# One of four block additions in a seven-product matrix multiplication done by an adding DMA, with the work of every half step laid out anew

## The chip, the cores and the metric

The kernel runs on one core of a Trainium2 chip, in float32. The metric is device time in microseconds (us) of one execution, as the median of several runs. Engines are named as in the profile: PE is TensorE (matmuls; PEld its weight loads), DVE is VectorE, ACT is ScalarE, POOL is GpSimd, and SP issues most of the DMAs.

## The reference

There are 16 batches (graphs) of 1024 nodes with 128 features, and two layers. The input adjacency is 0 or 1.

```python
# layer 0, per batch
h = x @ Ww.T + Wb
e = (h @ A) @ h.T;  e = e + e.T
attention = softmax(where(adj > 0, e, 0), axis=1) * adj
h_prime = relu(attention @ h)
ic, fc, oc = sigmoid(h_prime @ w?_u + x @ w?_x)      # three gates per node
x = layernorm(x + oc * tanh(ic * h_prime + fc * x))
# layer 1, per batch and head (4 heads)
h = x @ conv_w[hd] + conv_b[hd]
scores = h @ attn_w[hd] @ h.T
hh = relu(tanh(adj * scores) @ h)
x = layernorm(x + relu(relu(mean(hh over heads)) + x))
```

## The kernel before

Nodes are cut into 8 blocks of 128 rows, and rows of 1024 columns into 2 halves of 512. The main loop runs over the 16 batches `b`. In iteration b the kernel does layer 1 of batch b, and spread between its steps it does the end of layer 0 of batch b+1, the beginning of layer 0 of batch b+2 (pieces with a leading `+` in the plan), and the end of layer 1 of batch b-1 (`e`).

**Layer 1 in steps.** A batch has 4 heads x 8 steps. Two steps make a `Pair` (`i` = 0 to 3 in a head): a step multiplies one block of 128 rows by the head's matrix to get 128 x 1024 scores (two matmuls of 128 x 512 into PSUM, from a ring of three score buffers), DVE multiplies them by the adjacency out of PSUM into the pair's SBUF tile (L821 for the first half of the pair, L819 with a factor -1 for the second), and ACT takes tanh of the 128 x 1024 (L826).

**Seven products.** In batches 0 to 14, heads 0 to 2 are "fast": the product of the tanh matrix with h is done as a 2 x 2 block product with seven multiplications in place of eight (Winograd's form). The pair tile has five parts of 512 columns, in the order X3, N21, B22, B11, N12. The first half's scores fill B11 and N12, the second half's fill N21 and B22. Four block additions follow on DVE: `differ` makes X3 = N12 + B22 and N12 = N12 + B11 in one instruction of 1024 columns (L830), `differ_more` makes B22 = B22 + N12 (L892) and then N21 = B22 + N21 (L893). The seven products (L853) are

- P1: B11 with a block of h; P2: N21 as it was with h; P3: B22 as it was with hx; these are "early", and they sum in one PSUM tile over the four pairs of a head;
- P5: the new N12 with hx; P7: X3 with h; P4: the new N21 with h; P6: the new B22 with hx; these are "late", in another PSUM tile.

hx are three sums and differences of h's blocks that POOL makes (`join_rows`, L786 to L789). At the end of a head, `early_second` copies the early sums out of PSUM on ACT (L902, L905), `combine` joins them with the late ones on DVE (L912 to L917), `sum_up` adds on POOL (L924) and takes relu on ACT (L928, L930), and `sum_end` adds the head to the sum on POOL (L936). Head 3 and batch 15 multiply plainly (L865 in the fast batches).

**When a pair is worked on, before.** Pair p of a batch has its scores in steps 2p and 2p+1. The main loop holds two older pairs, `before` (p-1) and `old` (p-2). `differ` comes at the end of step 2p+2, the early products in step 2p+3 (P3 and P2 behind the first 512 scores, P1 behind the second), `differ_more` at that step's end, and the late products in step 2p+4 (P5, P7 behind the first 512 scores, P4, P6 behind the second).

**What sets the order.** There is no scheduler: each engine works through its instructions in the order in which the Python code issues them. The other work is laid out by hand in `PLAN` (and `FIRST` for b = 0), 64 strings for a batch's 64 half steps. `slot(n)` runs the pieces of string n: 2 x step after the first 512 scores of a step, 2 x step + 1 at its end. The pieces that the texts below name are: L load an adjacency block on SP; S scores of layer 0 and T their transposition through DRAM (a "hop": SP writes, and `land` reads back at the end of the step); E finds the edges (L466, POOL, 128 x 1024); A masks (L483, DVE) and takes exp (ACT); B weighs (L516, DVE) and multiplies; P to V are the gates and the normalization of layer 0. Of the gates, `weigh_hp` multiplies on POOL (L610), `sum_hp` sums on DVE (L616, L618), and `forget` multiplies x by the forget gate on POOL (L629, 128 x 1024). r and u make h and the head's matrix for layer 1, j calls `join_rows`, D turns the new x. The batch's output goes out by a DMA that POOL issues (L1033).

Of the kernel before, what the change touches and what calls it, by code (L numbers as in the profile page):

```python
# [15 lines left out]
ALU = mybir.AluOpType  # L16
# [3 lines left out]
P = 128  # L20
# [4 lines left out]
def two_layer_adjacency_kernel(  # L25
# [19 lines left out]
    nc = tc.nc  # L45
    B, N, D = x.shape
    H = conv_w.shape[0]
    assert D == P and N % 512 == 0
    NB = N // P
    NH = N // 512  # L50
    BH = NB // NH
# [287 lines left out]
    def layer0(b):  # L339
# [5 lines left out]
        t = {}  # L345
# [280 lines left out]
        def forget():  # L626
            t["u"] = sb.tile([P, NB, D], F32, tag="u", name=f"u0_{b}", bufs=1)
            t["x1"] = sb.tile([P, NB, D + 1], F32, tag="x1", name=f"x1_{b}")
            nc.gpsimd.tensor_mul(  # L629
                t["u"], t["x"], t["gate"][:, :, 1:2].to_broadcast([P, NB, D])  # L630
            )
            nc.gpsimd.memset(t["x1"][:, :, 0:1], 1.0)

        def gate_f():
# [61 lines left out]
        else:  # L696
            pieces.update(
                P=turn_hp, Y=partial(weigh_hp, 1), F=gate_f, f=gate_f_end, i=gate_i, o=gates_io,
# [104 lines left out]
    class Pair:  # L803
# [30 lines left out]

        def product(self, p):
            b, hd, i = self.b, self.hd, self.i
            if i == 0 and p == 3:
                early = ps_acc.tile([P, N], F32, tag="acc1", name=f"early_{b}_{hd}")
                acc1_t[b, hd] = {2: early[:, :HN], 1: early[:, HN:512], 3: early[:, 512 : 512 + HN]}
                acc1_t[b, hd, 0] = early  # L840
            if i == 0 and p == 5:
                late = ps_acc.tile([P, N], F32, tag="acc2", name=f"late_{b}_{hd}")
                for n, r in enumerate((5, 7, 6, 4)):
                    acc1_t[b, hd][r] = late[:, ts(n, HN)]
            out = acc1_t[b, hd][p]
            h, x = h1_t[b, i // 2][:, i % 2], hx_t[b, hd, i // 2][:, :, i % 2, :]
            d1, d2 = slice(hd * D, hd * D + HD), slice(hd * D + HD, (hd + 1) * D)
            w, at = {
                1: (h[:, 0, d1], B11), 2: (h[:, 1, d1], N21), 3: (x[:, 2], B22),
                4: (h[:, 1, d2], N21), 5: (x[:, 0], N12), 6: (x[:, 1], B22), 7: (h[:, 0, d2], X3),  # L850
            }[p]
            for q in range(NH):
                nc.tensor.matmul(  # L853
                    out[ts(q, HD)], w, self.t[:, at, ts(q, HN)],
                    start=(i == 0 and p in (2, 3, 5, 4)), stop=(i == BH - 1),
                    skip_group_check=True,
                )

# [16 lines left out]
                for e in range(2):  # L875
                    add_head(b, hd, acc1_t[b, hd][:, ts(e, 512)], e * 512)

        def late_first(self):
            self.product(5)
            self.product(7)  # L880

        def late_second(self):
            self.product(4)
            self.product(6)

        def early_first(self):
            self.product(3)
            self.product(2)

        def differ_more(self):  # L890
            t = self.t
            nc.vector.tensor_add(t[:, B22], t[:, B22], t[:, N12])  # L892
            nc.vector.tensor_add(t[:, N21], t[:, B22], t[:, N21])  # L893

        def early_second(self):
            self.product(1)
            if self.i < BH - 1:
                return
            b, hd = self.b, self.hd
            w = acc1_t[b, hd, 1] = sb.tile([P, 6, HN], F32, tag="w", name=f"w_{b}_{hd}", bufs=1)  # L900
            early = acc1_t[b, hd, 0]
            nc.scalar.copy(  # L902
                w[:, 4::-4, :], early[:, :512].rearrange("p (k n) -> p k n", k=2)
            )
            nc.scalar.copy(w[:, 5, :], early[:, 512 : 512 + HN])  # L905

        def combine(self):
            if self.i < BH - 1:
# [199 lines left out]
    for g in range(2):  # L1108
# [2 lines left out]


    PLAN = [
        "u1.1 B2", "B3", "A4 L5", "", "E5 r2 B4 r3", "r6 A5", "", "L6 E6", "L7 A6",
        "E7 u1.0 e B5", "", "r7", "B6 A7 j0.1", "B7", "", "e", "R0", "G0 G1 j1.0 j1.1",
        "G2 G3 G4", "+W", "G5 e", "G6 e", "G7 R1 e", "e P u2.0", "e +L0", "+E0 +H0 +h0", "",
        "j2.0", "+Q0", "u2.1 e", "Y", "+L1 +Q1", "+H1 +h1", "e X F", "u3.0 j2.1", "+S0 f", "+T0",
        "+H2 +h2 i +S1 +T1", "+S2 j3.0", "+T2 +S3", "o", "+S4 I0", "I1", "+T3 +S5", "", "",
        "+E1 O0", "u3.1", "+A0 O1", "+S6", "+B0 +L2 Va", "Vb Vc", "", "j3.1 Vd +T4 +L3 N0",
        "D +S7", "+A1", "+E2", "+T5", "+A2", "+B1 +E3", "", "", "r5 u0.1 u0.0 r4 +A3 r0 r1",  # L1120
        "+T6 +L4 +E4 j0.0",
    ]

    FIRST = [
        "A0", "B0 S5 L3", "E1 A1", "u1.1 E2 T3", "S6 T4 E3", "B1 A2 L4", "B2 u1.0 L5 T5", "E4 A3",
        "", "B3", "A4", "B4 E5", "S7 L6 L7 T6", "A5", "", "j1.1", "", "E6 X B5 E7", "A6 j1.0",
        "B6 A7 +W", "B7", "", "R0", "G0 G1 G2 G3 G4 G5", "G6 u2.1 G7 +L0", "+E0 +H0 +h0 R1", "P",
        "", "+Q0", "", "", "u2.0 +L1 +Q1", "j2.0 +H1 +h1", "Y F", "", "+S0", "j2.1 +T0",
        "+H2 +h2 f +S1 +T1", "+S2", "i +T2 +S3", "u3.0", "+S4", "u3.1 o", "+T3 I0 +S5", "",
        "O0 I1", "+E1", "j3.0 O1", "+A0 j3.1", "+S6 Va", "+B0 +L2", "Vb Vc", "Vd", "N0 +T4 +L3",  # L1130
        "D +S7", "+A1", "+E2", "+T5", "+A2", "+B1 +E3", "", "", "r1 u0.1 r4 +A3 r0 u0.0 r5",
        "+T6 +L4 j0.0 +E4",
    ]
    begun.append(True)
    end, nxt, ended = None, second, None
    pairs = deque([None, None])
    for b in range(B):
        plan = PLAN if b else FIRST
        after = layer0(b + 2) if b + 2 < B else {}

        def slot(n):
            for name in plan[n].split():
                if name == "e":
                    if end is not None:
                        next(end, None)
                elif name == "D":
                    if b + 1 < B:
                        turn_x1(b + 1)
                elif name[0] in "rju":
                    c = b + (n >= H * NB if name[0] == "r" else name[1] == "0" and n >= H * NB)  # L1150
                    if c == B:
                        continue
                    if name[0] == "r":
                        rows(c, (int(name[1]),))
                    elif name[0] == "j":
                        join_rows(c, int(name[1]), int(name[3]))
                    else:
                        head_uT(c, int(name[1]), [int(name[3])])
                elif name[0] == "+":
                    run(after, name[1:])  # L1160
                else:
                    run(nxt, name)

        for step in range(H * NB):
            hd, m = divmod(step, NB)
            i, half = divmod(m, 2)
            old, before = pairs
            if b + 1 < B:
                if half == 0:
                    now = Pair(b, hd, i)  # L1170
                for q in range(NH):
                    now.score(half, q)
                    if half == 0 and old and old.fast:
                        (old.late_second if q else old.late_first)()
                    if before and not before.fast:
                        before.plain(half, q)
                    elif half and before:
                        (before.early_second if q else before.early_first)()
                    if half and q == 0 and old and old.fast:
                        old.combine()  # L1180
                    if q == 0:
                        slot(2 * step)
                now.tanh(half)
                if half and before and before.fast:
                    before.differ_more()
            else:
                now = None
                layer1_step(b, hd, m)
                slot(2 * step)
                if half == 0 and old and old.fast:  # L1190
                    old.late_first()
                    old.late_second()
                if before and not before.fast:
                    before.plain(half, 0)
                    before.plain(half, 1)
                elif half and before:
                    before.early_first()
                    before.early_second()
                    before.differ_more()
                if half and old and old.fast:  # L1200
                    old.combine()
            if half == 0 and before and before.fast:
                before.differ()
            land()
            if half and old and old.fast:
                old.sum_up()
            if half == 0 and ended and ended.fast:
                ended.sum_end()
            slot(2 * step + 1)
            if step > H * NB - NB and b + 1 < B:  # L1210
                load_adj1(b + 1, ORDER[m - 1])
# [4 lines left out]
            if half:  # L1216
                ended = old
# [65 lines left out]
```

## Time and profile before

| | |
|---|---|
| runs | 2413.98 us median of 3 (2413.82 to 2415.39) |
| the execution profiled | 2419.07 us |
| its span, first to last instruction | 2417.2 us, mean granted TensorE clock 0.999 |
| L821, L819 DVE, scores times adjacency, 128 x 512 | 480 each, 677 and 679 ns |
| L826 ACT, tanh, 128 x 1024 | 480, 1056 ns |
| L853 PE, late and early products | 5 groups of 720 or 1440 records, 379 to 384 ns |
| L466 POOL, edges | 120, 2945 ns |
| L610 POOL, weighing | 45, 2496 ns |
| L629 POOL, forget gate | 15, 1908 ns |
| L513 ACT, multiplication of 128 x 128 by a column | 124, 398 ns |
| L1033 POOL, issue of the output DMA, 512 KB | 15, 1.01 us; 3.9 to 4.5 us from issue to landing |
| DMA traffic | 261 MB, mean 108 GB/s |

The page gives, for each group of instructions, the busy time in all, the mean time of one, and the idle time of the engine just before them with what ended most of it. A matmul has two records per instruction, and the two instructions of one 128-column matmul work on the two halves of the array at once; their ends are modelled, so the mean of a record is longer than the time for which it holds PE. The batches from 1 to 13 are alike, with a period of 147.5 to 149.0 us.

### The profile page before, as it was taken

The numbers are of one execution on the slowest core, as the hardware profiler recorded it, in microseconds if no ns is written. First come the engines' busy times: TensorE is split into PE (matmuls) and PEld (weight loads), VectorE is DVE, ScalarE is ACT, GpSimd is POOL, SyncE is SP. The second block draws the span as 40 slices with busy tenths as digits, with TensorE's granted clock in tenths as the row PEclk, the third lists the DMA queues.
The fourth block names the chain that finished last, engine by engine and source line by source line (L and its number), as shares of the span: only waits on it lengthen the run. The fifth ranks groups of instructions, "written<-read, shape, count | busy, mean of one in ns | idle before, by whom it ended". The sixth has DMA issues, their size and how long they took to land.

```text
span 2417.2 us, 37283 instructions
## 1 busy us (share of the span) xinstructions
PE 2364.2 (98%) x13817; PEld 1016.6 (42%) x13817; DVE 2032.3 (84%) x3682; ACT 1215.1 (50%) x1992; POOL 963.1 (40%) x713
## 2 busy tenths in 40 slices
PE   9899999999999999999999999999999999999999
PEld 5343433434354343544435434343443434434334
DVE  7888897988889888998888979889798897988645
ACT  6545454554545545455454554545445454564443
POOL 1544444444344443445434354344444434444100
PEclk9999999999999999999999999999999999999999
DMA  4525243452524425235252343524335243441200
GB/s 141 131 71 157 79 114 114 102 158 72 132 95 118 151 76 151 84 98 162 76 169 79 104 133 90 163 79 106 122 97 157 79 127 101 109 154 44 88 27 9
DMA packets 461783, 260.98 MB, mean 108 GB/s; under 512 B 387107, under 2 KB 412450, under 8 KB 461603
## 3 DMA queue, kind: packets, MB, share of 16 engines
q1 hardware_dynamic: 459149, 250.68, 36.9%
q0 software_dynamic: 2160, 7.87, 1.1%
q8 instruction: 109, 1.79, 0.3%
q14 instruction: 71, 0.58, 0.1%
q10 hardware_dynamic: 294, 0.07, 0.0%
HBM read 199.04 MB, written 59.51 MB: 107 GB/s over the span
## 4 chain that ended last, share of the span: by engine, by line
PE 63%; DVE 30%; DMA 2%; issue 2%; ACT 1%; POOL 1%; SPq 0%; DVEq 0%; POOLq 0%; ACTq 0%
PE sc L78 24%; PE acc L78 10%; PE late L853 8%; PE acc L865 6%; PE early L853 5%; DVE pair L819 4%; DVE pair L830 4%; PE pR L78 4%; DVE pair L821 3%; PE pT_u L78 3%; DVE pair L893 3%; DVE pair L892 3%; DVE turn L441 2%; DVE hws L616 2%; DVE R L483 2%
## 5 line engine op out<-in xcount | busy, mean ns | idle before, releaser
L78 PE MATMUL sc<-uT,x1T 128*64 128x512 f32 x4096 | 1057.5, 595 | 17.9 <-DVE h L402 5.1
L826 ACT ACTIVATE pair<-pair 128x1024 f32<-128x1024 f32 x480 | 506.7, 1056 | 581.0 <-DVE pair L821 332.5
L78 PEld LDWEIGHTS sc<-uT,x1T 128*64 128x64 f32 x4096 | 292.0, 137 | 448.3 <-issue 231.3
L819 DVE SCALAR_TENSOR_TENSOR pair<-sc,adj 128x512 f32<-128x512 f32 x480 | 321.2, 679 | 170.7 <-PE sc L78 169.1
L466 POOL TENSOR_SCALAR edge<-ring 128x1024 uint8<-128x1024 f32 x120 | 352.9, 2945 | 272.8 <-DMA ring<-in_adjT_dram 248.5
L821 DVE TENSOR_TENSOR pair<-sc,adj 128x512 f32<-128x512 f32 x480 | 318.0, 677 | 72.5 <-PE sc L78 70.7
L865 PE MATMUL acc<-pair,h 128*64 128x512 f32 x960 | 248.1, 594 | 0.0
L78 PE MATMUL acc<-R,h 128*64 128x512 f32 x960 | 240.5, 592 | 3.2 <-issue 1.6
L495 ACT ACTIVATE R<-R,nmax 128x1024 f32<-128x1024 f32 x126 | 144.5, 1147 | 195.1 <-DVE nmax L491 191.1
L853 PE MATMUL late<-pair,h 128*64 128x256 f32 x1440 | 221.0, 384 | 15.3 <-DVE pair L893 13.5
L241 POOL TENSOR_TENSOR rs<-rs,mhalf 128x8 f32<-128x8 f32 (+3 forms) x35 | 54.1, 1546 | 432.0 <-DVE rs L238 431.9
L830 DVE TENSOR_TENSOR pair<-pair 128x1024 f32<-128x1024 f32 x180 | 225.8, 1254 | 0.0
L853 PE MATMUL late<-pair,hx 128*64 128x256 f32 x1440 | 218.3, 380 | 0.1
L853 PE MATMUL early<-pair,h 128*64 128x256 f32 x1440 | 217.8, 379 | 0.0
L483 DVE CUSTOM_DVE_ANT_0 R<-R,edge 128x1024 f32<-128x1024 f32 x120 | 168.4, 1403 | 7.5 <-POOL edge L466 6.0
L893 DVE TENSOR_TENSOR pair<-pair 128x512 f32<-128x512 f32 x180 | 164.9, 916 | 6.2
L924 POOL TENSOR_TENSOR w<-w 128x512 f32<-128x512 f32 x45 | 57.4, 1275 | 279.1 <-ACT hpT L538 215.9
L853 PEld LDWEIGHTS late<-pair,h 128*64 128x64 f32 x1440 | 101.1, 137 | 157.7 <-DVE pair L893 71.2
L853 PEld LDWEIGHTS late<-pair,hx 128*64 128x64 f32 x1440 | 105.9, 137 | 127.0 <-issue 92.6
L853 PEld LDWEIGHTS early<-pair,h 128*64 128x64 f32 x1440 | 105.9, 137 | 126.3 <-issue 101.5
L516 DVE TENSOR_TENSOR R<-R,ring 128x1024 f32<-128x1024 f32 x120 | 154.8, 1290 | 0.0
L892 DVE TENSOR_TENSOR pair<-pair 128x512 f32<-128x512 f32 x180 | 149.4, 830 | 0.0
(215 smaller groups left out, 2939.6 us busy)
## 6 DMA issues: line engine op xcount, KB each, us to landing
adj<-in_adjT_dram SPq DMA_DIRECT2D x128, 512.0 KB, 4.5
ring<-in_adjT_dram SPq DMA_DIRECT2D x120, 512.0 KB, 4.9
xT<-in_xT_dram SPq DMA_DIRECT2D x16, 512.0 KB, 4.8
x<-in_x_dram SPq DMA_DIRECT2D x16, 512.0 KB, 7.6
dram_hp<-turn_hp SPq DMA_DIRECT2D x15, 512.0 KB, 2.9
hp<-dram_hp SPq DMA_DIRECT2D x60, 128.0 KB, 3.2
dram_x<-turn_x SPq DMA_DIRECT2D x15, 512.0 KB, 2.8
x1T<-dram_x SPq DMA_DIRECT2D x60, 128.0 KB, 4.0
```

Source lines behind the costliest of these rows:

```text
L78: nc.tensor.matmul(out[ts(c, HD)], lhsT[:, ts(c, HD)], rhs, start=start, stop=stop)
L466: engine.tensor_scalar(m, t["adj", j], 0.0, None, ALU.is_gt)
L483: nc.vector.tensor_tensor_reduce(to[:, ks], s[:, ks], t["edge", j][:, ks], 1.0, nmax, ALU.mult, ALU.max, top)
L516: nc.vector.tensor_mul(s[:, ks], s[:, ks], adj[:, ks])
L819: nc.vector.scalar_tensor_tensor(to, psv, -1.0, adj, op0=ALU.mult, op1=ALU.mult)
L821: nc.vector.tensor_mul(to, psv, adj)
L826: nc.scalar.activation(s, s, AF.Tanh)
L830: nc.vector.tensor_add(t[:, X3 : N12 + 1 : N12 - X3, :], t[:, N12 : N12 + 1, :].to_broadcast([P, 2, 512]), t[:, B22 : B11 + 1, :],)
L853: nc.tensor.matmul(out[ts(q, HD)], w, self.t[:, at, ts(q, HN)], start=(i == 0 and p in (2, 3, 5, 4)), stop=(i == BH - 1), skip_group_check ...
L865: nc.tensor.matmul(acc1_t[b, hd][ts(q, HD), ts(e, 512)], h1_t[b, i // 2][:, i % 2, half, d : d + HD], self.t[:, at : at + 2, ts(q, HN)], s ...
L892: nc.vector.tensor_add(t[:, B22], t[:, B22], t[:, N12])
L893: nc.vector.tensor_add(t[:, N21], t[:, B22], t[:, N21])
```

## The change

- `forget`: in the batches from 1 on, eight multiplications of 128 x 128 on ACT take the place of one of 128 x 1024 on POOL.
- `differ_more`: the addition into N21 is no longer DVE's L893 but a DMA that POOL issues, which reads B22 and adds it to N21 (256 KB).
- The products come in another order and later. The early ones are now in step 2p+2 (P1 behind the first 512 scores, P2 and P3 behind the second), the late ones in step 2p+5 (P4, P6 behind the first, P5, P7 behind the second). `combine` comes at the end of the step of the last late products, `sum_up` and `sum_end` one and two steps later.
- `differ` and `differ_more` are no longer at fixed places: they are pieces `d0` to `d15` and `m0` to `m15` of the plan, by pair (for the pairs of head 3 they do nothing). For each fast pair, m stands between the last early product and P4, with two to two and a half steps to P4.
- All 64 strings of both plans are new. They hold the same pieces, and d and m; B2 of a batch has moved to the end of the iteration before (`+B2`).

```diff
         def forget():
...
-            nc.gpsimd.tensor_mul(
-                t["u"], t["x"], t["gate"][:, :, 1:2].to_broadcast([P, NB, D])
-            )
+            for k in range(NB):
+                nc.scalar.mul(t["u"][:, k, :], t["x"][:, k, :], t["gate"][:, k, 1:2])
             nc.gpsimd.memset(t["x1"][:, :, 0:1], 1.0)
...
-            if i == 0 and p == 3:
+            if i == 0 and p == 1:
                 early = ps_acc.tile([P, N], F32, tag="acc1", name=f"early_{b}_{hd}")
...
-            if i == 0 and p == 5:
+            if i == 0 and p == 4:
                 late = ps_acc.tile([P, N], F32, tag="acc2", name=f"late_{b}_{hd}")
...
-                    start=(i == 0 and p in (2, 3, 5, 4)), stop=(i == BH - 1),
+                    start=(i == 0 and p in (1, 3, 5, 4)), stop=(i == BH - 1),
...
-        def late_first(self):
-            self.product(5)
-            self.product(7)
-
-        def late_second(self):
-            self.product(4)
-            self.product(6)
-
-        def early_first(self):
-            self.product(3)
-            self.product(2)
-
         def differ_more(self):
             t = self.t
             nc.vector.tensor_add(t[:, B22], t[:, B22], t[:, N12])
-            nc.vector.tensor_add(t[:, N21], t[:, B22], t[:, N21])
-
-        def early_second(self):
-            self.product(1)
+            nc.gpsimd.dma_start(t[:, N21], t[:, B22], accum_op=ALU.add)
+
+        def keep_early(self):
             if self.i < BH - 1:
                 return
...
+        def early(self, half, q):
+            if half:
+                return
+            for p in (2, 3) if q else (1,):
+                self.product(p)
+            if q:
+                self.keep_early()
+
+        def late(self, half, q):
+            if not half:
+                return
+            for p in (5, 7) if q else (4, 6):
+                self.product(p)
...
     PLAN = [
-        "u1.1 B2", "B3", "A4 L5", "", "E5 r2 B4 r3", "r6 A5", "", "L6 E6", "L7 A6",
-        "E7 u1.0 e B5", "", "r7", "B6 A7 j0.1", "B7", "", "e", "R0", "G0 G1 j1.0 j1.1",
-        "G2 G3 G4", "+W", "G5 e", "G6 e", "G7 R1 e", "e P u2.0", "e +L0", "+E0 +H0 +h0", "",
-        "j2.0", "+Q0", "u2.1 e", "Y", "+L1 +Q1", "+H1 +h1", "e X F", "u3.0 j2.1", "+S0 f", "+T0",
-        "+H2 +h2 i +S1 +T1", "+S2 j3.0", "+T2 +S3", "o", "+S4 I0", "I1", "+T3 +S5", "", "",
-        "+E1 O0", "u3.1", "+A0 O1", "+S6", "+B0 +L2 Va", "Vb Vc", "", "j3.1 Vd +T4 +L3 N0",
-        "D +S7", "+A1", "+E2", "+T5", "+A2", "+B1 +E3", "", "", "r5 u0.1 u0.0 r4 +A3 r0 r1",
-        "+T6 +L4 +E4 j0.0",
+        "L5 B3 A4", "d15", "E5", "B4", "m15", "L6 d0", "L7 m0 r7", "e r2", "u1.0 r3 d1 +W",
+        "A5 r6 E6", "E7 m1 j0.1 X", "B5", "u1.1", "j1.0 d2", "m2", "A6", "A7 u2.0 d3", "m3 B6",
+        "", "+L0", "B7", "", "d4 e R0 m4", "d5 G0 G1 +L1 +E0 G2 G3 e e", "e", "m5 G4 j1.1", "G5",
+        "", "j2.1 e G6 G7 R1 P j2.0 d6", "u2.1 m6", "e", "e", "d7", "+Q0 +H0 +h0", "m7",
+        "e +Q1 Y +S0 d8 +T0", "+S1 F", "f", "m8 i", "+S2", "+T1 j3.0 +H1 +L2", "d9", "+h1 m9",
+        "o +S3", "d10 u3.0 +T2 I0", "m10 +E1 u3.1", "", "+S4 O0 +H2 I1 +h2", "+T3 +T4 +S5",
+        "d11 +S6 m11 O1", "Va Vb", "Vc d12", "Vd j3.1", "+T5 +S7", "m12 N0 +A0 D", "", "d13 +B0",
+        "+A1 +E2", "+L3 m13", "+E3", "d14 +B1 +L4", "+T6 +A2", "+E4 u0.0 m14 r4 +B2 u0.1 r5",
+        "r1 r0 j0.0 +A3",
     ]
...
+                if name[0] in "dm":
+                    pair = int(name[1:])
+                    pair = pair_t.get((b - (n < 4 * pair + 3), pair))
+                    if pair and pair.fast:
+                        (pair.differ if name[0] == "d" else pair.differ_more)()
...
+        def products(half, q):
+            if old and old.fast:
+                old.late(half, q)
+            if before:
+                (before.early if before.fast else before.plain)(half, q)
...
                 for q in range(NH):
                     now.score(half, q)
...
+                    products(half, q)
                     if q == 0:
                         slot(2 * step)
                 now.tanh(half)
...
             land()
             if half and old and old.fast:
-                old.sum_up()
-            if half == 0 and ended and ended.fast:
-                ended.sum_end()
+                old.combine()
+            if ended and ended.fast:
+                (ended.sum_end if half else ended.sum_up)()
             slot(2 * step + 1)
```

`FIRST` is laid out anew in the same way.

## Prediction

> **What bounds the kernel now.** I read the page's busy shares and chain first, then the chain in order of time over one batch.
>
> ```profile
> PE 2364.2 (98%) x13817; PEld 1016.6 (42%) x13817; DVE 2032.3 (84%) x3682; ACT 1215.1 (50%) x1992; POOL 963.1 (40%) x713
> PE 63%; DVE 30%; DMA 2%; issue 2%; ACT 1%; POOL 1%; SPq 0%; DVEq 0%; POOLq 0%; ACTq 0%
> ```
>
> ```profile
> 1004.70 2.58 PE acc L78 x12
> ...
> 1037.16 0.88 PE sc L78 x4
> 1038.07 0.69 DVE pair L821
> 1038.76 1.13 DVE pair L830
> ...
> 1044.49 2.75 DVE pair L893
> ...
> 1083.38 0.70 DVE pair L893
> 1084.08 0.04 issue
> 1084.13 1.08 PE late L853 x8
> ```
>
> TensorE is the bound, but 98% is not its peak: the ends of matmuls are modelled. In an unbroken stretch 12 records 512 wide take 2.58 us, 0.215 each. All records of the trace, counted by width (256 wide as half, records of 128 output columns twice), are 10,768 such, so 10,768 x 0.215 = 2315 us. The span of 2417.2 thus holds 102 us in which TensorE was held up. The same count by stretch: 28 us before 203, 58.5 in the thirteen alike batches up to 2129 (4.5 each, of 148.2), 9 in the next, 7 after. No change that leaves the products as they are gains more. From 1038 to 1084 the chain runs on VectorE: there it is the limit. By stretch of this batch:
>
> ```profile
> core 0: us, PE busy (x) PEld busy (x) DVE busy (x) ACT busy (x) POOL busy (x), PEclk, DMA share, GB/s
> 950.00:1000.00 50.00, 48.77 (x266) 22.46 (x264) 39.48 (x64) 27.60 (x47) 24.81 (x21) 1.00 0.49 152
> 1000.00:1037.00 37.00, 37.00 (x248) 19.10 (x246) 29.71 (x55) 16.25 (x27) 14.37 (x12) 1.00 0.29 74
> 1037.00:1084.20 47.20, 45.60 (x294) 19.58 (x292) 45.84 (x82) 23.06 (x35) 14.95 (x11) 1.00 0.37 93
> ```
>
> From 1037 on DVE is busy 45.84 of 47.2 us while TensorE's records come to 202 x 0.215 = 43.4: 3.8 us lost, most of the batch's 5. Then the groups, and DVE and POOL in that stretch:
>
> ```profile
> L830 DVE TENSOR_TENSOR pair<-pair 128x1024 f32<-128x1024 f32 x180 | 225.8, 1254 | 0.0
> L893 DVE TENSOR_TENSOR pair<-pair 128x512 f32<-128x512 f32 x180 | 164.9, 916 | 6.2
> L892 DVE TENSOR_TENSOR pair<-pair 128x512 f32<-128x512 f32 x180 | 149.4, 830 | 0.0
> ```
>
> ```profile
> 1042.99 1.47 DVE L892 TENSOR_TENSOR pair<-pair 128x512 f32<-128x512 f32 x1
> 1044.49 2.75 DVE L893 TENSOR_TENSOR pair<-pair 128x512 f32<-128x512 f32 x1
> ```
>
> ```profile
> 1042.00 1.91 POOL L629 TENSOR_TENSOR u<-x,gate 128x1024 f32<-128x1024 f32 x1 [3.63 <-DVE gate L624]
> 1043.84 0.12 POOL L632 MEMSET x<- 128x8 f32 x1
> 1043.91 2.77 POOL L610 TENSOR_TENSOR x1T<-hp,wu_b 128x1024 f32<-128x1024 f32 x1
> ```
>
> L893, the addition that leaves, has a median of 0.69 us and a mean of 0.92: it ends late where POOL works.
>
> **What the skill says.** "SBUF — State Buffer", Who interferes with whom: a VectorE instruction with two SBUF inputs and a GpSimd one that reads SBUF block each other whole. The trace agrees: L892 and L893 above end when POOL's L629 and L610 end. "DMA: Bandwidth & Descriptors", SWDGE vs HWDGE vs iDMA: accumulating is open to GpSimd's DMAs alone, and all queues share the DMA engines. The trace has 15 POOL DMAs (L1033, 512 KB, no addition). The same page, Anatomy of one DMA: 2.0 us plus bytes by 436 KB a us. An estimate from it is 2.6 us for 256 KB; the trace has 3.9 to 4.5 from issue to landing for L1033's 512 KB, where it gives 3.2.
>
> **The change part by part.**
>
> *L893 goes from DVE.* 180 x 0.916 = 165 us, 11 a batch, of it 4 x 0.69 + 2.75 = 5.5 us in the stretch that DVE binds. What is late next is read from the load: I took the instructions of a middle batch in the built program's order, each at its row's median, and summed by four steps (32 in a batch). DVE against TensorE before: 15.0/17.6, 18.8/17.2, 17.5/21.5, 14.6/16.1, 18.7/20.4, **18.7/15.2, 18.5/15.7**, 13.8/19.8. After: 14.1/15.0, 13.4/17.2, 18.2/19.8, 14.2/17.2, 14.9/19.8, **18.9/17.6**, 15.7/16.3, 18.0/20.6. TensorE's sum is 143.5 in both, DVE's falls from 135.7 to 127.4 (medians, without the collisions). Before, DVE's excess in steps 20 to 27 is 6.3 us and cost 3.8: the three score buffers in PSUM let 2.5 pass. After, the worst run of steps (19 to 26, summed step by step) has 3.6, so 1.1 stays: **2.7 us a batch gained.**
>
> *L629 goes from POOL to ACT.* 1.91 us a batch less on POOL, and one collision (0.8 us on L892 above) less on DVE. ACT gets 8 x 0.40 (L513, same shape) = 3.2 us, in steps 17 and 18, between two tanhs. I cost it at nothing: ACT is 50% busy and a half's tanh is wanted about a step (4.5 us) later. Without that cover it is up to 3.2 a batch. Behind the eight stands the tanh of that step.
>
> *The adding DMA on POOL.* 180 issues by 1.01 us (L1033's own) = 182 us, 12 a batch; POOL goes from 62.5 to 72.7 of 148, still idle half the time. It waits for the addition into B22 (L892, L879 after); behind it on POOL stand edges (2.95 us), hx (four, 3.0 us) and weighings (2.5), for which masks, P3 and DVE's L616 wait. Ahead of it the same ones stand: behind an edge it goes up to 3 us late. SP issues none of it; its loads and hops share the engines with 180 x 256 KB = 47 MB beside 261.
>
> *Who waits for it: P4.* Before, P4 came second of the late products in step 2p+4 and waited for L893 (13.5 us on PE, 71.2 on the weight loads). Now it opens step 2p+5. From the place of the addition before the DMA to P4, TensorE has 6.4 to 9.7 us of other work (median about 7.3). Of this DVE takes the multiplication ahead and the addition, 0.68 + 0.69. That leaves 5.0 at the tightest and 5.9 at the median for POOL and transfer. The trace does not show an adding DMA. From below 2.6 (the page); from above 8 (twice L1033, as both operands are read and ring loads share the engines). I take 4.0, since half the bytes and two reads make about L1033's traffic. Then some 2 us are over at the median, of which DVE's own lag (up to 2.5 in the bound stretch) and POOL's queue take most: I put 1.0 us a batch. P4's wait before was about 1.2 (13.5 over 15 batches is 0.9, and some of the weight loads' 71.2 is not covered by matmuls), so **0.2 gained.** At 2.6 it would be about 1; at 8, with half a us of DVE lag, a pair loses 2.2, 26 us a batch. Behind P4 stand P6 and then, on PE in order, everything else.
>
> *The products' order, combine and sums.* The same 7 products, 0.43 us each; P1 first needs the first half's tanh only. Two steps later P4 and P6 open and P5 and P7 close. Combine follows a step later, with a step before the next head writes "late". Price 0; without that step it is its four DVE additions, 1.9 us a head.
>
> *The plans.* No piece is added or dropped; loads, hops and SP's issues move with their pieces. Steps 4 to 7 lose their DVE excess (18.8/17.2), in which TensorE lost little. The hops on SP keep seven or more half steps before their readers. A wait at a batch's head (1.4 us in one of four batches looked at) stays. I take -1 to +1 us a batch, 0 in the sum; L629's collision is inside the 2.7.
>
> **The sum.** 2.7 + 0.2 - 0.9 for the fresh waits that I don't see (a fifth of the old 4.5) = 2.0 a batch, x 13 = 26; batch 0 (7 us lost from 100 to 203, same DVE stretch) 3; batch 14 (9 lost, 2 of them P4's wait at 2230, where the clock was halved for 3.4 us) 2. 31 us: the profiled span goes from 2417 to 2386. The execution profiled took 2419.1 (1.9 us around the span), 5.1 over the median; a difference passes to the median as it is: 2414 - 31 = **2383**.
>
> **The rivals.**
> 1. *All cover holds.* The DMA lands in 3 us, DVE never binds: 4 of 4.5 us a batch come back, 52, plus 7: **2355**. For it: DVE's load is under TensorE's in all blocks but one. Against: single steps of 5.8/4.7 and 5.1/3.7.
> 2. *P4 waits for the DMA (slower).* Place: the first late product of each pair; price: every us that addition-to-landing is over its cover is lost 180 times, since each pair stands alike. It decides from a mean loss of 31/180 = 0.17 us, reached, with half a us of lag, when issue to landing is some 5.5 us. At 6.3 the loss is about 0.5: +90 - 31, **2473**. For it: no adding transfer in the trace, 5.0 us of cover at the tightest, POOL's edges ahead of it. Against: 4.0 to 4.5 for twice the bytes.
> 3. *The relief is spent elsewhere.* ACT's 3.2 us delay a tanh, and POOL's order makes hx late for P3 (in the third pair of head 0 it ends just as P3 comes). 2 us a batch: **2412**, no change.
>
> **Chances.** Forecast 0.50 (its own range 2368 to 2400), rival 1 0.18, rival 2 0.22, rival 3 0.10. A measurement here tells 0.2% (4.8 us) from no change. Faster: 0.50 + 0.18 + 0.04 of rival 3 = 0.72; same 0.05; slower 0.22 + 0.01 = 0.23. The range starts at 2354 and goes to 2445, which leaves out the worse half of rival 2 and a little of rival 1.
>
> **What would show it.** After: no L893 row; L879 at 0.69 to 0.83 us; DVE near 1,870 us busy; POOL near 1,120; the adding DMA landing 3.5 to 4.5 us after its issue; "late" waiting for a DMA less than 15 us in all; the DVE part of the chain under 15%. Wrong: a landing over 5.5 us, "late" waiting for a DMA by tens of us, or ACT before DVE among P2's and P1's waits.

## The result and the profile after

The changed kernel takes **2413.76 us** (median of 12 runs, 2412.25 to 2419.49) against 2414.96 for the kernel before on the same chip (12 runs). The ratio is 0.9999, 95% interval 0.9989 to 1.001: no change. The execution profiled took 2419.19 us, its span 2417.4, the mean granted clock 0.998. The forecast of 2383 was 31 us too low, and its own range, 2368 to 2400, was missed. The time is that of rival 3 (2412); whether its mechanism is too is settled below.

The page after, busy shares and chain:

```profile
PE 2346.7 (97%) x13817; PEld 1007.2 (42%) x13817; DVE 1967.7 (81%) x3502; ACT 1258.7 (52%) x2112; POOL 1025.9 (42%) x878
PE 77%; DVE 11%; ACT 3%; issue 2%; POOL 0%; POOLq 0%; ACTq 0%; DVEq 0%
```

VectorE did fall off the chain, from 30% to 11%, as forecast, and yet nothing was won. But its busy time fell by 65 us only, where the addition that left had taken 165. The groups say where most of the other 100 us came back (columns: busy us and mean ns of one, then the idle time before it):

```profile
L829 DVE TENSOR_TENSOR pair<-pair 128x1024 f32<-128x1024 f32 x180 | 261.5, 1453 | 16.9 <-ACT pair L825 16.9
...
L879 DVE TENSOR_TENSOR pair<-pair 128x512 f32<-128x512 f32 x180 | 124.0, 689 | 1.8 <-PE early L852 0.2
...
L618 DVE TENSOR_TENSOR gate<-hws,gate 128x8 f32<-128x8 f32 x45 | 37.3, 828 | 1.6
...
L623 DVE TENSOR_SCALAR gate<-gate 128x8 f32<-128x8 f32 x15 | 29.8, 1985 | 4.2 <-ACT gate L622 4.2
```

The addition into B22 that stayed (L892, now L879) is clean: 689 ns, before 830. In its place three others are slow: `differ` (L830, now L829) rose from 1254 to 1453 ns on average; L618, an addition of 128 x 8 in the gates, has a median of 172 ns and a mean of 828; L623, which adds 1 to 128 x 8 in the sigmoid of the forget gate, takes 1985 ns on average, about that in each of 15 batches, where it took 174 before. Against the kernel before these are 36, 25 and 27 us more. Two other groups got longer too, L516 by 15 us and the last sums of layer 1 (L1027, L1029) by 20; no wait of TensorE stands at either.

The adding DMA, by its source line (who waited for it, us and times; then issue to landing):

```profile
  PEld late L852: 4.4, 3
  PE late L852: 2.9, 1
...
DMA to landing us min/median/max: 3.2/3.8/6.0
```

PE waited for it once in 180 pairs, in batch 0. Before, "late" had waited for L893 13.5 us on PE and 71.2 on the weight loads.

By stretch of a middle batch, cut at other half steps than the stretches shown before, since the work lies elsewhere:

```profile
core 0: us, PE busy (x) PEld busy (x) DVE busy (x) ACT busy (x) POOL busy (x), PEclk, DMA share, GB/s
944.50:996.00 51.50, 51.50 (x272) 19.33 (x270) 42.74 (x66) 29.37 (x48) 30.43 (x22) 1.00 0.68 200
996.00:1035.00 39.00, 39.00 (x244) 17.39 (x242) 33.29 (x60) 15.98 (x24) 15.55 (x20) 1.00 0.25 56
1035.00:1070.00 35.00, 31.62 (x214) 14.40 (x212) 30.64 (x40) 20.46 (x39) 15.67 (x11) 1.00 0.60 123
1070.00:1092.40 22.40, 22.40 (x152) 10.43 (x148) 18.91 (x55) 12.78 (x23) 6.49 (x5) 1.00 0.65 147
```

Three stretches have no gap in TensorE at all; from 1035 to 1070 it stands for 3.4 us by its records, and 4.4 by the prediction's count (records x 0.215). The thirteen alike batches lose 55.8 us so counted, before 58.5. So the loss on DVE's old stretch is gone, and a new one of nearly the same size stands in one place of each batch.

That place in order of time (start us, duration us, engine, line; in brackets the idle time before it and what ended that):

```profile
1043.51 3.74 DVE L829 TENSOR_TENSOR pair<-pair 128x1024 f32<-128x1024 f32 x1 [1.13 <-ACT pair L825]
...
1043.68 2.47 POOL L610 TENSOR_TENSOR x1T<-hp,wu_b 128x1024 f32<-128x1024 f32 x1
...
1048.90 1.08 PE L78 MATMUL sc<-uT,x1T 128*64 128x512 f32 x4 [1.02 <-DVE pair L820]
...
1050.05 2.37 POOL L610 TENSOR_TENSOR x1T<-hp,wu_b 128x1024 f32<-128x1024 f32 x1 [3.84 <-DVE hws L616]
...
1050.46 1.98 DVE L623 TENSOR_SCALAR gate<-gate 128x8 f32<-128x8 f32 x1 [0.28 <-ACT gate L622]
...
1054.29 2.43 ACT L630 ACTIVATE u<-x,gate 128x128 f32<-128x128 f32 x8
...
1056.42 1.08 PE L78 MATMUL sc<-uT,x1T 128*64 128x512 f32 x4 [0.85 <-DVE pair L818]
...
1064.62 2.65 POOL L936 TENSOR_TENSOR sum<-sum,w 128x1024 f32<-128x1024 f32 x1
...
1065.17 2.14 DVE L618 TENSOR_TENSOR gate<-hws,gate 128x8 f32<-128x8 f32 x1
...
1067.87 1.08 PE L78 MATMUL pT_u<-x1T,ms 128*64 128x512 f32 x4 [1.37 <-ACT R L423]
```

Read it in threes. A POOL instruction with two SBUF inputs runs (L610, L610, L936); a DVE instruction that meets it ends when POOL's ends or takes that much longer (L829 3.74 us where it takes 1.22 alone at 1060.48; L623 1.98 for 0.17, ending at 1052.44 when L610 ends at 1052.42; L618 2.14 for 0.17); then TensorE stands, because the scores' multiplication L820 or L818 queues behind the DVE instruction, or ACT's L423 behind an exponential that waits for L618. It fits the shared port that the prediction cited from the Trainium skill ("SBUF — State Buffer", Who interferes with whom). The page also counts a `tensor_scalar` in its two-port mode among the instructions that take the port; L623 is one of 128 x 8 and is held up, though no run here shows in which mode it ran. By the trace L829 starts 0.17 us ahead of L610 and is held all the same. The third L610 of the batch (1055.74, 2.62 us) delays nobody: beside it run L818 (0.69 us) and the four additions of `combine` (0.41 to 0.69), each with one of its inputs in PSUM.

Counted from matmul to matmul, TensorE loses 1.19 us at 1048.90, 1.02 at 1056.42 with 0.31 at 1058.08, and 1.54 at 1067.87: 4.06 of the 4.4. What a diff can show of each: piece `Y` (the first L610) stands in the same half step as `d8` (`differ`); `F` (sum and sigmoid of the forget gate) is followed at once by `f`, where the second L610 stood behind `forget` on POOL until that left for ACT; `o`, which issues L618, comes when `sum_end` (L936) of a head is due.

### The profile page after: what moved, and what is told of

Its sections match the earlier page's. It is cut to its first block, busy times and chain, and to the rows that moved or that the text cites. A ratio compares the mean times of both kernels' runs of the same rounds, so it can differ in the third digit from the quotient of the medians.

```text
span 2417.4 us, 37970 instructions
## 1 busy us (share of the span) xinstructions
PE 2346.7 (97%) x13817; PEld 1007.2 (42%) x13817; DVE 1967.7 (81%) x3502; ACT 1258.7 (52%) x2112; POOL 1025.9 (42%) x878
## 3 DMA queue, kind: packets, MB, share of 16 engines
q8 instruction: 109, 1.79, 0.3%
## 4 chain that ended last, share of the span: by engine, by line
PE 77%; DVE 11%; ACT 3%; issue 2%; POOL 0%; POOLq 0%; ACTq 0%; DVEq 0%
PE sc L78 32%; PE acc L78 10%; PE late L852 10%; PE acc L864 9%; PE early L852 7%; PE pT_u L78 4%; PE pR L78 4%; DVE pair L829 2%; DVE hws L616 1%; DVE gate L618 1%; DVE pair L818 1%; DVE pair L820 1%; ACT pair L825 1%; DVE gate L623 1%; PE pR_h L78 1%
## 5 line engine op out<-in xcount | busy, mean ns | idle before, releaser
L880 POOL DMA_DIRECT2D pair<-pair x180 | 160.6, 892 | 827.5 <-PE sc L78 217.2
L818 DVE SCALAR_TENSOR_TENSOR pair<-sc,adj 128x512 f32<-128x512 f32 x480 | 326.4, 685 | 116.7 <-PE sc L78 115.2
L466 POOL TENSOR_SCALAR edge<-ring 128x1024 uint8<-128x1024 f32 x120 | 365.6, 3051 | 108.1 <-DMA ring<-in_adjT_dram 61.7
L820 DVE TENSOR_TENSOR pair<-sc,adj 128x512 f32<-128x512 f32 x480 | 323.7, 680 | 106.5 <-PE sc L78 105.6
L829 DVE TENSOR_TENSOR pair<-pair 128x1024 f32<-128x1024 f32 x180 | 261.5, 1453 | 16.9 <-ACT pair L825 16.9
L516 DVE TENSOR_TENSOR R<-R,ring 128x1024 f32<-128x1024 f32 x120 | 170.2, 1419 | 0.0
L483 DVE CUSTOM_DVE_ANT_0 R<-R,edge 128x1024 f32<-128x1024 f32 x120 | 154.3, 1285 | 1.0 <-POOL edge L466 1.0
L78 PE MATMUL pT_u<-x1T,ms 128*64 128x512 f32 x504 | 130.2, 595 | 18.1 <-ACT R L423 17.8
L610 POOL TENSOR_TENSOR x1T<-hp,wu_b 128x1024 f32<-128x1024 f32 x45 | 112.0, 2489 | 56.6 <-DVE hws L616 56.6
L78 PE MATMUL sc<-xT,qT 128*64 128x512 f32 (+3 forms) x684 | 129.3, 484 | 0.3 <-ACT R L423 0.2
```

The lines of the kernel that those rows point to most:

```text
L78: nc.tensor.matmul(out[ts(c, HD)], lhsT[:, ts(c, HD)], rhs, start=start, stop=stop)
L466: engine.tensor_scalar(m, t["adj", j], 0.0, None, ALU.is_gt)
L483: nc.vector.tensor_tensor_reduce(to[:, ks], s[:, ks], t["edge", j][:, ks], 1.0, nmax, ALU.mult, ALU.max, top)
L516: nc.vector.tensor_mul(s[:, ks], s[:, ks], adj[:, ks])
L818: nc.vector.scalar_tensor_tensor(to, psv, -1.0, adj, op0=ALU.mult, op1=ALU.mult)
L820: nc.vector.tensor_mul(to, psv, adj)
```

## The experiments

**The theories**, by the numbers that the expectations use. *Theory 1, collisions*: the change gave what it promised, and the three meetings take it back; each, taken away alone, gives back its own stall in each batch (1.2, 1.3 and 1.5 us). *Theory 2, DVE's load*: DVE has too much to do in steps 19 to 26 whatever POOL does, and a stall that is taken away comes back elsewhere. *Theory 3, ACT's cost* (rival 3): the eight multiplications on ACT delay tanh, and putting them back on POOL is a gain. An adding DMA that lands late for P4 is left nothing by the lines above. Each run stands beside runs of the kernel before on the same chip, whose medians were 2416.93, 2417.17 and 2415.58 in the three groups; ratios are to those. The changed kernel did not run beside them; that it takes as long as the kernel before (0.9999) is carried over from the result.

### Take away one meeting at a time

`e1_weigh_early`: the first L610 issued one half step earlier.

```diff
-        "", "j2.1 e G6 G7 R1 P j2.0 d6", "u2.1 m6", "e", "e", "d7", "+Q0 +H0 +h0", "m7",
-        "e +Q1 Y +S0 d8 +T0", "+S1 F", "f", "m8 i", "+S2", "+T1 j3.0 +H1 +L2", "d9", "+h1 m9",
+        "", "j2.1 e G6 G7 R1 P j2.0 d6", "u2.1 m6", "e", "e", "d7", "+Q0 +H0 +h0", "Y m7",
+        "e +Q1 +S0 d8 +T0", "+S1 F", "f", "m8 i", "+S2", "+T1 j3.0 +H1 +L2", "d9", "+h1 m9",
```

> PLAN alone: Y (the first weighing on POOL, L610) from half step 35 to 34, ahead of m7's DMA, so that it no longer runs while DVE adds for d8 (L829, 3.74 us in place of 1.2). Theory 1 (collisions of DVE with POOL in the gate stretch took the gain): L829 goes back to 1.2 us there, the stall of 1.2 us before the scores at 1049 goes, 14 batches x 1.2 = 17 us faster. Theory 2 (DVE has too much to do in steps 19 to 26 whatever POOL does): the stall moves on, under 5 us gained. Theory 3 (ACT's eight multiplications): no change.

Measured: 2397.47, ratio 0.9918 (0.9902 to 0.9934), -19.5 us. The stall ahead of L820 is gone. L610 now delays the addition L879 in 11 of 15 batches (1.87 to 2.88 us for 0.68); in two of these TensorE stands for 0.75 us afterwards, in the others not at all.

`e2_one_on_act`: the 1 of the sigmoid added on ACT.

```diff
-            nc.vector.tensor_scalar_add(gate, gate, 1.0)
+            nc.scalar.activation(gate, gate, AF.Identity, bias=1.0)
```

> The + 1 of the sigmoid (L623, 128x8, 1.98 us beside POOL's second L610 in place of 0.18) goes from DVE to ACT. Theory 1: the stalls of 1.0 and 0.3 us at 1056 and 1058 go, 14 x 1.3 = 18 us faster, DVE's busy time 30 us lower. Theory 2: under 5 us. Theory 3: slower by a few us, as ACT gets 30 more instructions of 0.2 us in the same stretch.

Measured: 2396.64, ratio 0.9914 (0.9899 to 0.9929), -20.3 us. On ACT it takes 0.21 us, and the two stalls of 1.0 and 0.3 are gone; the third grew from 1.54 to 1.79.

`e3_o_early`: `o`, and L618 with it, two half steps earlier, ahead of the sum instead of beside it.

```diff
-        "e +Q1 Y +S0 d8 +T0", "+S1 F", "f", "m8 i", "+S2", "+T1 j3.0 +H1 +L2", "d9", "+h1 m9",
-        "o +S3", "d10 u3.0 +T2 I0", "m10 +E1 u3.1", "", "+S4 O0 +H2 I1 +h2", "+T3 +T4 +S5",
+        "e +Q1 Y +S0 d8 +T0", "+S1 F", "f", "m8 i", "+S2", "+T1 j3.0 +H1 +L2", "d9 o", "+h1 m9",
+        "+S3", "d10 u3.0 +T2 I0", "m10 +E1 u3.1", "", "+S4 O0 +H2 I1 +h2", "+T3 +T4 +S5",
```

> PLAN alone: o (sum and sigmoid of the last two gates) from half step 43 to 41, so that its addition L618 (2.14 us) no longer stands beside POOL's L936. Theory 1: L618 goes to 0.2 us, the stall of 1.5 us before pT_u at 1068 goes, 14 x 1.5 = 21 us faster. Theory 2: under 5 us. Theory 3: nothing, as the stall hangs on ACT's evacuations.

Measured: 2418.22, ratio 1.0003 (0.9994 to 1.0013): a miss. L618 was freed (0.17 us each of three times in a middle batch), but L936 ran all the same, and another met it. The timeline of this kernel, one batch:

```profile
1070.25 2.66 POOL L936 TENSOR_TENSOR sum<-sum,w 128x1024 f32<-128x1024 f32 x1
...
1071.40 2.61 DVE L829 TENSOR_TENSOR pair<-pair 128x1024 f32<-128x1024 f32 x1
```

`differ` takes 2.61 us for 1.2 here, and L665 some microseconds later 1.1 more than alone. To move this victim in time handed POOL's reading to the next one.

`e4_all` is the three together, `e7_two_and_o_late` the first two with `o` one half step later (and `I0` two later):

```diff
-        "o +S3", "d10 u3.0 +T2 I0", "m10 +E1 u3.1", "", "+S4 O0 +H2 I1 +h2", "+T3 +T4 +S5",
+        "+S3", "d10 u3.0 +T2 o", "m10 +E1 u3.1", "I0", "+S4 O0 +H2 I1 +h2", "+T3 +T4 +S5",
```

> The three edits together. Theory 1: 4.0 us a batch in 14 batches, 50 to 57 us faster, near 2360, and TensorE is held up less than 1 us in a middle batch. Theory 2: new stalls in the same steps, under 15 us gained. Theory 3: under 15 us gained, with ACT before the stalls that are left.

> The first weighing earlier and the + 1 on ACT, as in the two runs that gained 20 us each, and o one half step later in place of earlier (I0 follows to half step 46). Theory 1: the two gains add up, 38 us; with o late L618 misses L936, d9's L829 may be hit in its place but no evacuation on ACT waits for it, so a further 5 to 20 us: 2357 to 2375. Theory 2 (DVE's load): no better than 2382.

Measured: 2382.38, ratio 0.9849 (0.9836 to 0.9863), and 2386.74, ratio 0.9878 (0.9859 to 0.9898). Both miss what theory 1 forecast, by 22 and by 12 us or more, and `e7_two_and_o_late` is no better than theory 2 allowed (2382). The alike batches still lose 2.3 us each in the one, where L936 lengthens `differ` as in the third experiment, and 2.6 in the other, where L653, which multiplies in the gates, meets POOL's L466 (2.64 us for 1.13) and a stall of 1.27 follows. The next runs decide between the two theories.

### Take POOL's reading away instead

L936 adds two operands of 512 KB; an adding DMA can do that too, and POOL then only issues it.

```diff
-            nc.gpsimd.tensor_add(sum_t[self.b], sum_t[self.b], w)
+            nc.gpsimd.dma_start(sum_t[self.b], w, accum_op=ALU.add)
```

`e10_sum_by_dma` is the changed kernel with this edit alone, `e9_two_and_sum_by_dma` with it and the edits of the first two experiments (`o` in its place).

> The changed kernel with L936 as an adding DMA and nothing else. Moving o only moved L936's collision to L829; with no read on POOL there is nobody to collide with. Theory 1: L618 at 0.2 us, L516 at the head of a batch 1 us shorter, the stall of 1.5 us before pT_u gone: 18 to 24 us faster. Theory 2: under 5 us.

> The two edits that gained 20 us each (first weighing earlier, + 1 on ACT), o at its old place, and the sum of the heads (L936, which POOL read for 2.4 us) as an adding DMA of 512 KB. Theory 1 (collisions): the third stall goes too, for nothing of POOL's reads beside L618; 38 + 21 us, near 2356. Theory 2 (DVE's load in steps 19 to 26): no better than 2382.

Measured: alone 2393.59, ratio 0.9911 (0.9895 to 0.9927), -22 us; together **2357.53**, ratio 0.9762 (0.9743 to 0.9782), 2.4% faster than the kernel before, and the best of the study. L618 in the first of them, by its source line (min, median, max):

```profile
L618 DVE TENSOR_TENSOR gate<-hws,gate x45: 170/172/174, 155.8 to 2217.7; 128x8 f32<-128x8 f32 x45
```

and the page of the second:

```profile
PE 2335.7 (99%) x13817; PEld 1014.3 (43%) x13817; DVE 1873.6 (79%) x3472; ACT 1264.4 (54%) x2142; POOL 982.1 (42%) x878
PE 94%; DVE 3%; DMA 1%; ACT 1%; POOL 0%; issue 0%; SPq 0%; POOLq 0%; DVEq 0%; ACTq 0%
```

No L618 is slow any more, and the chain is TensorE's to 94%. Alone the three edits gave 19.5, 20.3 and 22, together 58 us. In the profiled executions the thirteen alike batches lose 42.7, 40.3 and 34.9 us with one edit and 6.2 with all three, where the changed kernel loses 55.8: the parts, 13.1, 15.5 and 20.9, add up to the whole, and are near 13 times the stalls of 1.19, 1.33 and 1.54. *Theory 1* holds, in place and in size; theory 2, which allowed under 5 us for each and nothing better than 2382 for the three, falls.

### Undo one part of the change

`e5_forget_on_pool` puts the forget gate's multiplication back on POOL.

```diff
-            for k in range(NB):
-                nc.scalar.mul(t["u"][:, k, :], t["x"][:, k, :], t["gate"][:, k, 1:2])
+            nc.gpsimd.tensor_mul(
+                t["u"], t["x"], t["gate"][:, :, 1:2].to_broadcast([P, NB, D])
+            )
```

> One part of the change undone: the forget gate is POOL's one multiplication again (L629), in front of the second weighing L610. Theory 1 (collisions; taking L629 off POOL let the second L610 start right behind L616 and hit L623): L623 is back at 0.2 us, the second L610 starts some 4 us later, and L629 hits another two-input addition instead (L879); 5 to 18 us faster than the changed kernel. Theory 3 (ACT's eight multiplications delay tanh): 15 to 40 us faster. If the move to ACT was of use as it stands: slower.

Measured: 2445.16, ratio 1.0113 (1.0095 to 1.0131), 28 us **slower**: what theories 1 and 3 forecast had the sign wrong. Its timeline in one batch (lines are one higher here):

```profile
906.26 1.91 POOL L629 TENSOR_TENSOR u<-x,gate 128x1024 f32<-128x1024 f32 x1 [4.78 <-DVE gate L624]
...
908.18 2.76 POOL L610 TENSOR_TENSOR x1T<-hp,wu_b 128x1024 f32<-128x1024 f32 x1
...
910.97 1.22 DVE L616 TENSOR_REDUCE hws<-x1T 128x8 f32<-128x1024 f32 x1 [2.25 <-POOL x1T L610]
...
913.05 1.19 PE L78 MATMUL sc<-uT,x1T 128*64 128x512 f32 x4 [2.16 <-DVE pair L819]
```

L623 is indeed clean (175 ns), because L610 comes later, behind L629, which waits for the gate. But the next piece then issues DVE's L616, which waits for that L610, and DVE is in order: the scores behind it wait, and TensorE with them. After this stall its clock was halved for a while (the third column from the end):

```profile
914.30:917.70 3.40, 3.40 (x22) 2.09 (x20) 2.10 (x4) 0.73 (x2) 1.58 (x2) 0.56 0.13 50
```

The alike batches lose 6.5 us each on average. A collision was exchanged for a wait with the same start, which costs more. And *theory 3* falls: the eight on ACT are worth 28 us in this layout.

`e6_add_on_dve` is the changed kernel with the addition into N21 on DVE again, `e8_e7_add_on_dve` the same in the kernel of `e7_two_and_o_late`.

```diff
-            nc.gpsimd.dma_start(t[:, N21], t[:, B22], accum_op=ALU.add)
+            nc.vector.tensor_add(t[:, N21], t[:, B22], t[:, N21])
```

> The other part undone: in the changed kernel N21 is added by DVE again, no DMA. DVE gets 12 x 0.69 = 8.3 us a batch back, of it 4 in steps 19 to 26. If the relief was worth what the prediction's load sum said: about 2.7 us a batch, 35 to 40 us slower, near 2453. If collisions alone set the stalls (theory 1 in its strong form): under 10 us slower, as DVE has room outside them.

> The kernel before this one with N21 added by DVE again: what the adding DMA is worth once the collisions are out. By the load sum: 2.7 us a batch, 35 to 40 us slower than with the DMA. If DVE has room there: under 10 us slower.

Measured: 2439.63, ratio 1.0097 (1.008 to 1.0113), and 2417.82, ratio 1.0002 (0.9994 to 1.0011), against 2386.74 with the DMA. The adding DMA saves 24 and 31 us, less than the 35 to 40 of the load sum and more than the 10 of its rival. It is not DVE's load alone that it saves: in both kernels the addition on DVE takes 2.73 us for 0.69 once a batch, beside L936; in `e6_add_on_dve` TensorE stands for 1.77 us after it.

### Each part alone

`e11_plan_alone` has both edits back: what is left of the change is the plans and the order of the products. `e12_before_forget_on_act` is the kernel before with the eight multiplications on ACT, and nothing else.

> Both moved operations undone: DVE adds N21, POOL multiplies by the forget gate; the products' order and the plans stay. If the new layout by itself is what costs: the two parts were worth 26 and 31 us in it, so near 2417 + 57 = 2474 (less where both relieve the same stretch: from 2450). If the layout is neutral: 2417 to 2430.

> In the kernel before, only the forget gate goes from POOL to ACT. By the prediction's step (one collision of 0.8 us less, nothing for ACT): 5 to 12 us faster. If, as in the changed kernel, the second weighing then starts right behind L616 and hits L623 (2 us in place of 0.18): no gain or up to 15 us slower. In both cases L616's wait for the third weighing gets shorter.

Measured: 2465.23, ratio 1.0200 (1.018 to 1.022), 50 us slower than before; and 2410.16, ratio 0.9975 (0.9965 to 0.9986), 5.4 faster. In the latter L629's meeting with L892 is gone, and that of the L610 behind it with L893 (2.75 us), but this L610 now starts at once and meets L623: 2.0 us instead of 0.17. Much of what was taken from two DVE instructions went to a third, so the gain is at the lower edge of what the prediction's step gave (5 to 12).

The change taken apart, in us against the kernel before (ratio x 2416):

| | N21 added by DVE | by DMA |
|---|---|---|
| old layout, forget on POOL | 0 | not tried |
| old layout, forget on ACT | -5 | not tried |
| new layout, forget on POOL | +48 | +27 |
| new layout, forget on ACT | +23 | 0 |

So the new layout with DVE's addition and POOL's multiplication costs 48 to 50, the DMA gives 21 to 24 in it, the move to ACT 25 to 27. Where most of this loss stands is in the timeline of `e11_plan_alone` (the addition into N21 is L881 here, the heads' sum L937):

```profile
919.15 2.76 POOL L610 TENSOR_TENSOR x1T<-hp,wu_b 128x1024 f32<-128x1024 f32 x1
919.73 2.73 DVE L881 TENSOR_TENSOR pair<-pair 128x512 f32<-128x512 f32 x1
...
924.44 1.21 PE L78 MATMUL sc<-uT,x1T 128*64 128x512 f32 x4 [2.57 <-DVE pair L819]
...
932.08 2.85 POOL L937 TENSOR_TENSOR sum<-sum,w 128x1024 f32<-128x1024 f32 x1 [4.77 <-ACT w L931]
...
932.75 2.73 DVE L881 TENSOR_TENSOR pair<-pair 128x512 f32<-128x512 f32 x1
...
936.14 1.08 PE L78 MATMUL sc<-uT,x1T 128*64 128x512 f32 x4 [1.59 <-DVE pair L819]
```

They are meetings again, but others: L881 takes 2.73 us for 0.69 twice in every batch, and TensorE stands for 2.74 and 1.76 us (matmul to matmul) behind it; L618 and the L623 of the forget gate are clean in this run. The alike batches lose 7.6 us each, before 4.5. So the table's parts don't add up as costs of their own: the DMA and the move to ACT take away meetings that this layout makes with DVE's addition, and the kernel as changed has three of its own. The order of the products and the strings were not tried apart, nor the adding DMA in the old layout.

## Why the prediction was wrong

**The step that failed** is "The plans": "I take -1 to +1 us a batch, 0 in the sum; L629's collision is inside the 2.7", and with it the "Price 0" of the products' order and sums, as the plans and the new place of `sum_end` (L936) are not told apart by a run. In the kernel as changed three meetings take 4.06 us a batch, 53 us in the alike batches, and without them the kernel is 58 us faster. The prediction had read such a meeting in the trace before (L892 and L893 beside L629 and L610), yet compared the two layouts' load with each row at its median, "without the collisions". For the old layout it then took the old collisions away with L893 and L629; for the new one it never asked which DVE instructions would now stand beside L610 and L936. The window of steps that it watched, 19 to 26 (steps counted from a batch's start), was a matter of DVE's sum; the loss came in steps 17 to 22, two of the three meetings from instructions of 0.17 us. That gain and loss cancel to 0.1% is chance.

**A reading of the lines.** The prediction says that L892 and L893 end when L629 and L610 end. By its own lines they end 0.55 and 0.56 us later (1044.46 after 1043.91, 1047.24 after 1046.68): they are held until POOL is done and do most of their own 0.69 us then. That they are held is right.

**VectorE's relief was right in kind.** 2.7 us a batch and 5 us at the ends, some 40 us, were forecast for DMA and move together. The stretch on DVE's path is gone: the chain's share is 11%, forecast under 15%. The size is not measured by itself. Taken out of the new layout, the two are worth 48, but that holds the meetings of L881; with the three meetings out of the way the kernel stands 58 us under the kernel before, but that has three edits more.

**ACT at nothing was right, and its consequence was missed.** The eight took 2.43 us (0.30 each, not 0.40), in their place at 1054.29 a single stall of 0.3 us (1058.08) follows, and no tanh is late. What the prediction did not follow is the queue that they left: "1.91 us a batch less on POOL" also meant that the L610 behind L629 starts earlier, into L623: 0.1 us after L616's end, and 2.9 us after it where L629 stands ahead (`e5_forget_on_pool`). `e12_before_forget_on_act` shows the same in the old layout.

**The adding DMA** was priced at 4.0 us and lands in 3.8 (3.2 to 6.0); its issue was priced at 1.01 and takes 0.89. Rival 2 with its decision point of 5.5 us falls.

**P4's wait** was mis-sized: 0.2 us a batch was entered, and the late products' gaps on TensorE, counted from matmul to matmul, went from some 27 us in the run to 4, which is 1.6 a batch.

**"Fresh waits", 0.9 a batch**, was the right thought with the wrong size: 4.06.

**Rivals.** Rival 3 gave the time within 2 us by luck: its parts (a tanh delayed by ACT, hx late for P3) aren't in the trace, where the early products wait for tanh once, 0.5 us, and never for hx, and undoing its cause made the kernel slower. Rival 1, that all cover holds, gave 2355; the kernel without the three meetings takes 2357.5, though with three edits that the rival didn't have.

**What would show it**: DVE's busy time was the sign that failed, 1,968 for "near 1,870", and it is 1,874 in `e9_two_and_sum_by_dma`, where the three meetings are gone. POOL has 1,026 for 1,120: the issues are 22 us cheaper, and the hx additions took 57 us less in their new places. The waits for the DMA, forecast under 15 us, are 2.9 on PE and 4.4 on the weight loads.

## What to carry to other kernels

When work is laid out anew between VectorE and GpSimd, don't compare sums of medians: go through the new order and ask, for each GpSimd instruction that reads SBUF, which VectorE instruction with two SBUF inputs or in a two-port mode stands beside it, the tiny ones too, and who queues behind that. Taking GpSimd's reading away (an adding DMA, 22 us here) cured it where moving the victim only found another. An instruction that leaves a queue lets the ones behind it start earlier: follow those as well. And what a part is worth, taken out of one layout, holds for that layout: the 21 to 24 us of the DMA here include a meeting of the addition that it replaces.

## What was not expected of the hardware

- The size of a meeting doesn't follow the VectorE instruction's own: additions of 128 x 8 that take 0.17 us alone took 2.0 to 2.2 beside a GpSimd instruction of 2.4 to 2.65. A `differ` of 1.22 took 3.74.
- TensorE's clock was halved for 3.4 us after some stalls, and not after others of the same length: after the stall of 2.33 us (matmul to matmul) in 9 of 14 batches of `e5_forget_on_pool`, after the one of 2.75 in only 4 of 14 of `e11_plan_alone`. The Trainium skill ("TensorE: Matmul & The Clock Gate", Why this matters for your kernels) advises against gaps of over some 3 us; here 2.33 was enough. The traces show what decides. Within a trace the half clock starts at whole multiples of 3.413 us (in `e11_plan_alone` at 321.1, 925.3, 1379.2 and 1833.2: 177, 133 and 133 of them apart). With the time cut into stretches of that length, each of the 25 starts in the 14 traces, between the first 60 us and the kernel's end, follows a stretch in which TensorE, counted from matmul to matmul, stood for 2.17 us or more; in no other stretch at full clock did it stand for over 2.14. So a stall that falls across two stretches can pass. A batch with the half clock lost 1.5 us more than one without it (6.9 for 5.4 in `e5_forget_on_pool`, 8.6 for 7.1 in `e11_plan_alone`).
- An adding DMA from SBUF to SBUF took 3.8 us from issue to landing for 256 KB (median of 180, 3.2 to 6.0). The 512 KB of the heads' sum took 7.8 and 8.4 (medians of 30 in `e10_sum_by_dma` and `e9_two_and_sum_by_dma`, 5.4 to 11.3), where the plain 512 KB output takes 3.9 to 4.5.
